# A pairwise bilinear kernel: a third tile for weights loaded twelve pairs ahead, and fields loaded in twos

## The chip, the cores and the metric

One Trainium2 chip, one NeuronCore. The metric is device time in microseconds (us), median of several executions. All runs told here were of the fast state; the runs before of different chips have medians from 760.2 to 761.7 us, so each kernel is also compared with runs of the kernel before on its own chip.

## The reference

There are 1,024 rows of 32 fields with 128 values each, and 496 pairs of fields (i < j), each with its own 128x128 matrix:

```python
v_i = inputs[:, I_IDX, :]
v_j = inputs[:, J_IDX, :]
transformed = jnp.einsum('bpd,ped->bpe', v_i, W)
return transformed * v_j
```

Everything is float32. The output is 260 MB, the weights 32.5 MB, the fields 16.8 MB.

## The kernel before

Pairs are taken with i falling from 30 to 0. All 32 fields stay in SBUF once loaded (4 KB of each partition). For a pair, TensorE multiplies the field by the weights; from pair 15 on with three matmuls of split operands (ScalarE and GpSimd make the split parts). VectorE multiplies by the other field into an output tile of three pairs, and SyncE stores that tile, 1.5 MB in rows of 12 KB. Weights come in tiles of eight pairs, 512 KB in rows of 4 KB, two tiles in turn. Loads go from ScalarE's queue, apart from those of the start:

```python
WL = 8          # pairs in a tile of weights
OG = 3          # pairs in an output tile; four such tiles
WB = 2          # tiles of weights
WLEAD = 6
XLEAD = 5
...
def load_w(c, splits=(0, WL), eng=nc.scalar):
    w_raw[c] = rpool.tile([P, WL, P], F32, tag="w", name=f"w_{c}")
    for a, b in zip(splits, splits[1:]):
        eng.dma_start(out=w_raw[c][:, a:b, :], in_=wt[c, :, a:b, :])
...
w_at = {}
for c in range(WB, -(-NQ // WL)):
    free = (c - WB + 1) * WL if (c - WB) * WL < nq0 else 0
    w_at[max(c * WL - 3 * WC + 1 - WLEAD, free)] = c
...
for u in range(2 * NQ + LAG):          # u: half a pair
    q = u // 2
    if u < 2 * NQ:
        i, j = pairs[q]
        if u % 2 == 0 and j == i + 1 and 0 <= i - 2 - XLEAD:
            load_x(i - 2 - XLEAD, eng=nc.scalar)
        first(u)                        # two matmuls, ScalarE scales PSUM
        if u % 2 == 1 and q in w_at:
            load_w(w_at[q])
    if u >= LAG:
        second(u - LAG)                 # third matmul, VectorE, the store
    ...                                 # one split of weights or of half a field
```

## Time and profile before

| | before |
|---|---|
| median of 6 runs (range) | 761.69 us (760.32 to 763.02) |
| span of the profiled run | 758.7 us |
| HBM read, written | 49.3 MB, 260.0 MB |
| DMA queues busy, of 16 engines | 83.1% + 16.0% |
| ScalarE's wait for weights | 38.7 us, 39 times |
| VectorE's wait for a free output tile | 46.6 us, 49 times |

The page is read for two kinds of facts: how busy an engine is (shares), and who waited for whom. The prediction below shows the lines that carry it. Not shown there are the issues of DMA, on the same page (source and target, the issuing queue, count, KB each, median us from issue to landing):

```profile
out_dram<-ot SPq DMA_DIRECT2D x163, 1536.0 KB, 13.5
w<-in_wt_dram ACTq DMA_DIRECT2D x60, 512.0 KB, 9.0
x<-in_xt_dram ACTq DMA_DIRECT2D x24, 512.0 KB, 9.4
```

A store takes 13.5 us to land although its 1.5 MB move in under 4 us at 409 GB/s: several are queued one behind the other.

### The profile page before, as it was taken

How to read it: one execution, taken by the hardware profiler on the slowest of the kernel's cores; microseconds unless marked ns; L12 is line 12 of the kernel's file. 1: busy time of each engine (PE TensorE's matmuls, PEld its weight loads, DVE VectorE, ACT ScalarE, POOL GpSimd, SP SyncE). 2: the span in 40 equal slices, each digit the busy share in tenths (PEclk: the TensorE clock that was granted, in tenths of full speed). 3: DMA queues.
4: the chain of work that ended last, by engine and by line, in shares of the span. 5: the costliest groups of instructions: out<-in, count | busy, mean ns of one | idle time of the engine just before them, and what ended most of it. 6: DMA issues, size and time to landing. Idle time of an engine off the chain costs nothing.

```text
span 758.7 us, 11264 instructions
## 1 busy us (share of the span) xinstructions
PE 708.1 (93%) x2946; PEld 551.6 (73%) x2946; DVE 633.7 (84%) x1012; ACT 625.7 (82%) x1256; POOL 595.6 (78%) x863
## 2 busy tenths in 40 slices
PE   7979989999999999999998989999999999999992
PEld 3557778777777777777786878778787777777771
DVE  4869989987888779788797989888888888888883
ACT  1368889988888888888887979898899899989881
POOL 0959999999888987978878787888887878786650
PEclk9999999999999999999999999999999999999996
DMA  9999999999999999999999999999999999999996
GB/s 351 427 406 389 425 394 424 427 418 430 420 422 418 425 423 409 419 416 411 400 411 420 404 423 402 422 417 409 410 414 417 402 423 400 408 424 404 416 412 257
DMA packets 38800, 310.07 MB, mean 409 GB/s; under 512 B 4304, under 2 KB 4432, under 8 KB 17872
## 3 DMA queue, kind: packets, MB, share of 16 engines
q1 hardware_dynamic: 26064, 264.25, 83.1%
q10 hardware_dynamic: 12672, 45.09, 16.0%
q8 instruction: 24, 0.39, 0.2%
q14 instruction: 40, 0.33, 0.1%
HBM read 49.28 MB, written 260.05 MB: 408 GB/s over the span
## 4 chain that ended last, share of the span: by engine, by line
DMA 40%; PE 39%; DVE 12%; POOL 5%; issue 1%; ACT 1%; DVEq 0%; ACTq 0%; POOLq 0%
DMA out_dram<-ot 34%; PE po L162 24%; DVE ot L177 12%; PE po L171 12%; DMA w<-in_wt_dram 6%; PE po L159 4%; POOL xl L111 1%; POOL xd L116 1%; POOL wl L96 1%; POOL xl L112 1%; POOL wd L98 1%; ACT po L163 0%; DMA x<-in_xt_dram 0%; DVE xd L203 0%; POOL wd L97 0%
## 5 line engine op out<-in xcount | busy, mean ns | idle before, releaser
L177 DVE TENSOR_TENSOR ot<-po,x 128x512 f32<-128x512 f32 x992 | 619.8, 683 | 109.4 <-DMA out_dram<-ot 46.6
L163 ACT ACTIVATE po<-po 128x512 f32<-128x512 f32 x962 | 540.7, 582 | 58.6 <-PE po L162 24.4
L162 PE MATMUL po<-xh,wh 128*128 128x512 f32 x962 | 382.6, 398 | 13.6 <-DVE ot L177 12.9
L171 PE MATMUL po<-xd,wd 128*128 128x512 f32 x962 | 377.8, 393 | 12.6 <-ACT po L163 11.4
L162 PE MATMUL po<-xl,wl 128*128 128x512 f32 x962 | 378.7, 394 | 5.6 <-POOL wl L96 5.3
L96 POOL TENSOR_TENSOR wl<-w,wh 128x256 fp32r<-128x256 f32 x241 | 181.0, 751 | 76.0 <-ACT wh L95 62.2
L162 PEld LDWEIGHTS po<-xh,wh 128*128 128x128 f32 x962 | 181.8, 189 | 72.0 <-DVE ot L177 33.9
L171 PEld LDWEIGHTS po<-xd,wd 128*128 128x128 f32 x962 | 181.7, 189 | 54.0 <-POOL wd L97 5.7
L162 PEld LDWEIGHTS po<-xl,wl 128*128 128x128 f32 x962 | 182.0, 189 | 46.3 <-POOL wl L96 9.7
L98 POOL TENSOR_TENSOR wd<-wl,wd 128x256 fp32r<-128x256 f32 x241 | 178.4, 740 | 20.1
L95 ACT ACTIVATE wh<-w 128x256 fp32r<-128x256 f32 x241 | 99.8, 415 | 42.3 <-DMA w<-in_wt_dram 38.7
L97 POOL TENSOR_SCALAR wd<-wh 128x256 fp32r<-128x256 f32 x241 | 99.3, 412 | 20.3
L111 POOL TENSOR_TENSOR xl<-x,xh 128x512 fp32r<-128x512 f32 x52 | 69.2, 1331 | 18.6 <-ACT xh L110 18.3
L116 POOL TENSOR_TENSOR xd<-xh,xl 128x512 fp32r<-128x512 f32 x32 | 41.3, 1291 | 2.7
L110 ACT ACTIVATE xh<-x 128x512 fp32r<-128x512 f32 x52 | 32.6, 631 | 12.6 <-DMA x<-in_xt_dram 12.6
L112 POOL TENSOR_SCALAR xl<-xl 128x512 fp32r<-128x512 f32 x52 | 33.3, 641 | 4.6
L159 PE MATMUL po<-x,w 128*128 128x512 f32 x60 | 28.3, 634 | 4.5 <-DMA x<-in_xt_dram 4.5
L159 PEld LDWEIGHTS po<-x,w 128*128 128x128 f32 x60 | 11.8, 202 | 20.2 <-issue 13.0
L203 DVE TENSOR_TENSOR xd<-xh,xl 128x512 fp32r<-128x512 f32 x20 | 16.8, 838 | 3.6 <-POOL xl L112 3.6
L110 ACT ACT_TABLE_LOAD x1 | 1.3, 1283 | 4.6 <-DMA w<-in_wt_dram 4.6
L219 POOL MEMSET const-float32-0.0<- 128x1 f32 x1 | 0.1, 98 | 0.2 <-issue 0.2
L219 POOL MEMSET const-bfloat16-1.0<- 128x1 bf16 x1 | 0.1, 101 | 0.0
(2 smaller groups left out, 0.2 us busy)
## 6 DMA issues: line engine op xcount, KB each, us to landing
out_dram<-ot SPq DMA_DIRECT2D x163, 1536.0 KB, 13.5
w<-in_wt_dram ACTq DMA_DIRECT2D x60, 512.0 KB, 9.0
x<-in_xt_dram ACTq DMA_DIRECT2D x24, 512.0 KB, 9.4
x<-in_xt_dram SPq DMA_DIRECT2D x6, 512.0 KB, 8.5
out_dram<-ot SPq DMA_DIRECT2D x5, 512.0 KB, 11.0
x<-in_xt_dram ACTq DMA_DIRECT2D x4, 256.0 KB, 5.9
out_dram<-ot SPq DMA_DIRECT2D x4, 256.0 KB, 10.1
w<-in_wt_dram SPq DMA_DIRECT2D x1, 512.0 KB, 7.9
```

What stands on the lines that cost most here:

```text
L95: nc.scalar.mul(h, raw, 1.0 - 2.0**-13)
L96: nc.gpsimd.tensor_tensor(l, raw, h.bitcast(F32), ALU.subtract)
L97: nc.gpsimd.tensor_scalar(d, h.bitcast(F32), EPS, 1.0, ALU.mult, ALU.mult)
L98: nc.gpsimd.tensor_tensor(d, l.bitcast(F32), d.bitcast(F32), ALU.subtract)
L111: nc.gpsimd.tensor_tensor(l, x_sb[f][:, s], h.bitcast(F32), ALU.subtract)
L112: nc.gpsimd.tensor_scalar(l, l.bitcast(F32), 1.0 / EPS, 1.0, ALU.mult, ALU.mult)
L116: nc.gpsimd.tensor_tensor(d, h.bitcast(F32), l.bitcast(F32), ALU.subtract)
L159: nc.tensor.matmul(po[u], w_raw[q // WL][:, q % WL, :], x_sb[i][:, s], start=True, stop=True)
L162: nc.tensor.matmul(po[u], w_s[c][t][:, r], x_s[i][t][:, s], start=t == 0, stop=t == 1)
L163: nc.scalar.mul(po[u], po[u], 1.0 + EPS)
L171: nc.tensor.matmul(po[u], w_s[q // WC][2][:, r], x_s[i][2][:, s], start=False, stop=True, skip_group_check=True)
L177: nc.vector.tensor_tensor(ots[g][:, k, s], po.pop(u), x_sb[j][:, s], ALU.mult)
```

## The change

Its intent is that ScalarE never waits for weights: a third tile lets each load start about twelve pairs ahead. The room for it comes from field 0, which is needed last and as left operand only, and is now put into one of the three weight tiles late in the run. The other fields are loaded two at a time, so that a partition's row in HBM is 8 KB in place of 4 KB. Cut to its core (text after @@ says where a cut stands, "..." that lines are left out):

```diff
-WB = 2
-WLEAD = 6
+WB = 3
+WLEAD = 12
+XAFTER = 54
@@ load_x
-        t = xpool.tile([P, n, BT], F32, tag=f"x{f}", name=f"x_{f}")
+        if f == 0:
+            t = rpool.tile([P, WL, P], F32, tag="w", name="x_0").rearrange("p q e -> p (q e)").unsqueeze(1)
+        else:
+            t = xpool.tile([P, n, BT], F32, tag=f"x{f}", name=f"x_{f}")
@@ start, after the loads of the first eight fields
+    load_w(2, eng=nc.sync)
@@ w_at
-        w_at[max(c * WL - 3 * WC + 1 - WLEAD, free)] = c
+        early = 0 if XAFTER < c <= XAFTER + WB else WLEAD - 6
+        w_at[max(c * WL - 3 * WC - 5 - early, free)] = c
+    x_at = XAFTER * WL - 11
...
@@ main loop
-            if u % 2 == 0 and j == i + 1 and 0 <= i - 2 - XLEAD:
-                load_x(i - 2 - XLEAD, eng=nc.scalar)
+            f = i - 2 - XLEAD
+            if u % 2 == 0 and j == i + 1 and f > 0 and f % 2 == 1:
+                load_x(max(f - 1, 1), min(f, 2), eng=nc.scalar)
...
+            if u == 2 * x_at + 1:
+                load_x(0, eng=nc.scalar)
```

More of the change, by code (lines that the diff above doesn't have):

```diff
@@ L144 @@
         free = (c - WB + 1) * WL if (c - WB) * WL < nq0 else 0
-        w_at[max(c * WL - 3 * WC + 1 - WLEAD, free)] = c
+        early = 0 if XAFTER < c <= XAFTER + WB else WLEAD - 6
+        w_at[max(c * WL - 3 * WC - 5 - early, free)] = c
+    x_at = XAFTER * WL - 11
+    assert x_at not in w_at and len(w_at) == NQ // WL - WB
     ctx.enter_context(tc.manual_schedule())
```

## The prediction

> **What bounds the kernel now.** I read the page from the top, then the waits, then a table by stage, then the transfers.
>
> ```profile
> span 758.7 us, 11264 instructions
> ...
> PE 708.1 (93%) x2946; PEld 551.6 (73%) x2946; DVE 633.7 (84%) x1012; ACT 625.7 (82%) x1256; POOL 595.6 (78%) x863
> ...
> DMA  9999999999999999999999999999999999999996
> ...
> DMA packets 38800, 310.07 MB, mean 409 GB/s; under 512 B 4304, under 2 KB 4432, under 8 KB 17872
> ...
> q1 hardware_dynamic: 26064, 264.25, 83.1%
> q10 hardware_dynamic: 12672, 45.09, 16.0%
> ...
> DMA 40%; PE 39%; DVE 12%; POOL 5%; issue 1%; ACT 1%; DVEq 0%; ACTq 0%; POOLq 0%
> ```
>
> PE at 93% looks like the bound, but the two DMA queues together are busy 99.1% of the time of all 16 engines: q1 (SyncE's queue, nearly all of it output) 83.1%, q10 (ScalarE's, weights and fields) 16.0%. The longest part of the chain that ended last is also DMA. The waits show who waits for whom:
>
> ```profile
> POOL wl L96 <- ACT wh L95: 62.2, 85, 6.3
> DVE ot L177 <- DMA out_dram<-ot: 46.6, 49, 1.4
> ACT wh L95 <- DMA w<-in_wt_dram: 38.7, 39, 9.1
> DVE ot L177 <- PE po L171: 35.1, 44, 5.1
> ```
>
> Columns: total us, times, longest. Two of these are of interest. ScalarE waits 38.7 us for weights: this is what the change aims at. VectorE waits 46.6 us for an output tile to be free, so the compute is held back by the stores. Which of the two counts is settled by the table by stage (after the busy times: granted clock, DMA share, GB/s):
>
> ```profile
> 20.00:50.00 30.00, 25.25 (x78) 15.51 (x77) 21.15 (x34) 11.95 (x26) 21.18 (x28) 0.94 1.02 423
> 53.00:55.00 2.00, 2.00 (x11) 1.65 (x10) 2.00 (x4) 2.00 (x5) 1.85 (x3) 1.00 0.64 270
> 55.00:130.00 75.00, 71.32 (x301) 56.63 (x300) 72.41 (x112) 65.04 (x134) 68.76 (x94) 0.98 1.01 408
> 260.00:390.00 130.00, 124.20 (x527) 97.30 (x526) 107.75 (x176) 114.01 (x228) 107.81 (x159) 1.00 1.01 414
> 520.00:650.00 130.00, 127.16 (x549) 101.98 (x548) 110.84 (x182) 117.44 (x235) 104.91 (x157) 1.00 1.01 412
> 730.00:745.00 15.00, 14.15 (x60) 10.81 (x58) 14.47 (x24) 11.93 (x23) 5.65 (x9) 1.00 0.97 407
> ```
>
> The DMA share is 1.00 or more (neighbouring packets overlap by a few ns) in every stage but 53 to 55 us and the last 30 us. Counting stores between issue and landing in the trace, 2.0 are in flight on average from 20 to 130 us and 3.1 from 130 to 730 us. So the DMA engines always have something to write when a weight is late. The kernel is bound by the time its 310 MB take on 16 engines.
>
> **What the Trainium skill says.** "DMA: Bandwidth & Descriptors", section "Specifications", gives a fabric ceiling of 435 GB/s; the mean here is 409, so at most 6% is left. The same page, "Queues, rings and completion order", says that an engine takes turns between the queues with work, packet by packet; the trace agrees: while one load runs beside the stores, its packets start 612 ns apart, close to one 12 KB store packet (460 ns) and one 4 KB load packet (159 ns). A lead therefore reorders traffic and does not add capacity. "Where 436 GB/s comes from" and "Latency and other measured facts" (HBM access 0.2 us on average, 2 us under high load) on that page bear on the stretched load packets below: the longest here is 1.6 us.
>
> **The change part by part.** The order of work on TensorE, VectorE and GpSimd is the same before and after; on ScalarE only the places of loads and of the two field splits beside them move, and SyncE gets one more load. HBM bytes are unchanged.
>
> *8 KB rows.* The trace's packet records give medians of 460 ns for 12,288 B, 159 ns for 4,096 B, 9 ns for the 4 B packet that closes a transfer on each engine, and 309 ns for the few 8,192 B packets that are there (instruction fetches). So a packet costs some 8.5 ns plus 27.2 GB/s. Eleven pairs of fields are loaded together, 128 rows each: 1,408 packets save 2x159-309 = 9 ns, 12.7 us of engine time, over 16 engines 0.8 us. Eleven transfers fewer save 11x16x9 ns/16 = 0.1 us. Sum: -0.9 us.
>
> *Third weight tile, lead of twelve pairs.* Before, the load of a tile is issued about six pairs before its first split; six pairs of 1.5 us are 9 us, and the median landing is 9.0 us. So it lands just in time, and ScalarE waits a little 39 times. Six more pairs add 9 us of slack, and nearly all of the 38.7 us goes, and most of GpSimd's 62.2 us behind ScalarE that comes from it. But an idle ScalarE costs end time only where the stores run dry. Adding up in the trace the time in which fewer than 16 engines have a packet: 2.3 us in the first 4 us, 0.1 us from 4 to 20, 1.1 us from 20 to 130, 2.8 us from 130 to 730, 0.5 us from 730 to 748, the rest after the last data. The only gap of note is at 53.7 us (0.6 us, the 0.64 in the table). It follows a 5.8 us wait of ScalarE for weights that ended at 45.2 us and reached VectorE as a 5.1 us wait. That tile was asked for at 34.8 us (pair 16) and is now asked for at pair 8. So -0.6 us from that gap, and at most 1 us more from small ones, of which I count none.
>
> *Stretched packets.* Packets that took over 6 ns more than the straight line add up to 20.1 us (mean of the 16 engines): 0.6 before 20 us, 3.3 to 130, 4.9 to 390, 11.0 to 730. They come just after reads are issued: in the 0.8 to 4.5 us after a load of weights issued with no other read in flight, 0.31 us on average (41 loads); beside another read, 0.10 us (19 loads). Fields: 0.23 us alone (6), 0.12 us beside others (14). Eleven field loads fewer save about 11x0.15 = 1.7 us; some six weight loads lose the field load that covered them, 6x0.2 = +1.2 us. Net -0.5 us. The part after 390 us, where weights are loaded alone in both kernels, should stay.
>
> *Start and end.* One more weight tile goes on SyncE's queue ahead of the first stores, and a pair's second field comes a field early: about 1 MB, 2.4 us of DMA time, moved forward, none of it added. At the end the reads stop some six pairs earlier. There compute needs about 1.36 us a pair (0.68 us a half on TensorE), stores 1.25 us, so the backlog shrinks by 0.11 us a pair over 25 pairs instead of 19: 2.8 us of a backlog of about 11 us, so no new gap, but perhaps a little at the edges. I take 0.
>
> Sum: -0.9 -0.6 -0.5 = -2.0 us, 762.0 to 760.0 us.
>
> **The rivals.** (1) The weights' wait sets the pace. If ScalarE's 38.7 us were on the path, the time would fall to some 723 to 740. For it: TensorE is 93% busy, and VectorE waits for TensorE 35.1 us. Against it: the DMA share of 1.01, and the floor. Taking the 20.1 us of stretched packets and the 4.5 us of gaps from 4 to 748 us wholly away leaves about 737; no earlier weight can do all that. (2) Contention takes the gain back. An 8 KB row has 40% of the bytes beside a 12 KB store row, a 4 KB row 25%, so a field load pushes stores and, at the start, SyncE's own loads aside; with fewer reads left to fill in later, the stores, only two deep to 130 us, run dry more often. That would cost 1 to 2 us: 761 to 763. (3) Read stalls depend on how deep the reads are queued. If loads that no one waits for fall on better moments, half of the 8.2 us before 390 us could go, for 756 to 757; if the number of stalls is kept and each is longer for 8 KB rows, the time is 761. (4) The ring's slot that field 0 takes late puts three weight tiles back to the old lead: some small waits of ScalarE come back near 650 us, hidden as the others were.
>
> **Range and chances.** The runs before lie between 761.2 and 763.0, so a median is good to about 1 us. The terms are each below 1 us, with perhaps 3 us either way for stalls. Range 756.5 to 763.0, prediction 760.0. Faster by over 2% means below 746.8 and needs rival 1; slower by over 2% means above 777 and a new gap of 15 us, for which nothing speaks.
>
> **What would show it right or wrong.** Right: the wait of ScalarE for weights falls below 10 us, VectorE's wait for output tiles grows in exchange, the DMA share stays 0.99 or more, the gap at 53.7 us is gone, packets fall by about 1,600 and those of field pairs take 309 ns. Wrong in the first step if VectorE's wait for output tiles does not grow and the mean GB/s rises above 415; wrong on stalls if the stretched packets change by more than 4 us; wrong on the start if the first 130 us show new gaps.

## The result, and the profile after

The changed kernel took 757.50 us (6 runs, 757.36 to 757.79) against 761.69 us. The ratio is 0.9946, 95% interval 0.9933 to 0.9959. It is the mean time of one kernel's fast runs over that of the other's of the same rounds, so not quite the ratio of the two medians. That is 4.1 us less where 2.0 were predicted. Part of the 4.1 us is the draw: this median of the kernel before is the highest of the five on record, and beside 25 runs on another chip (below) the difference was 3.3 us. A second thing shows in the runs: those of the kernel before spread over 2.7 us, those of the changed one over 0.4 us.

The page of the changed kernel, the lines that answer to those of before:

```profile
span 755.8 us, 11316 instructions
...
PE 706.6 (93%) x2946; PEld 548.1 (73%) x2946; DVE 625.1 (83%) x1012; ACT 629.6 (83%) x1256; POOL 595.4 (79%) x863
...
DMA packets 37216, 310.07 MB, mean 410 GB/s; under 512 B 4128, under 2 KB 4256, under 8 KB 14880
...
q1 hardware_dynamic: 26208, 264.78, 83.6%
q10 hardware_dynamic: 10944, 44.57, 15.4%
...
DMA 52%; PE 23%; DVE 17%; POOL 3%; issue 1%; ACT 0%; DVEq 0%; POOLq 0%; ACTq 0%
```

The DMA queues are as full as they were (99.0% together), with 1,584 packets fewer. The chain that ended last moves further towards DMA (40% to 52%). Its waits (us in total, times, longest; line 100 is the split of weights on ScalarE, 186 VectorE's multiply):

```profile
POOL wl L101 <- ACT wh L100: 70.4, 96, 1.9
DVE ot L186 <- DMA out_dram<-ot: 61.9, 62, 2.6
ACT po L172 <- PE po L171: 51.5, 63, 10.8
...
ACT wh L100 <- DMA w<-in_wt_dram: 0.5, 1, 0.5
```

ScalarE's 38.7 us for weights are gone, and the same engine now waits 51.5 us for TensorE (24.4 before); VectorE waits 15 us more for output tiles. Idle time has moved, little of it has vanished: with the DMA queues full, work done earlier only waits later. By stage (us, busy of PE, PEld, DVE, ACT, POOL, granted clock, DMA share, GB/s):

```profile
20.00:50.00 30.00, 30.00 (x106) 19.64 (x105) 27.30 (x43) 16.88 (x37) 25.59 (x34) 1.00 1.02 427
53.00:55.00 2.00, 0.97 (x5) 0.45 (x3) 1.50 (x3) 1.59 (x4) 1.82 (x3) 1.00 0.98 414
55.00:130.00 75.00, 70.90 (x300) 55.48 (x301) 68.89 (x110) 65.45 (x133) 69.24 (x94) 1.00 1.01 425
520.00:650.00 130.00, 127.12 (x546) 100.88 (x545) 111.28 (x182) 117.39 (x234) 103.22 (x155) 1.00 1.00 413
```

The stage from 55 to 130 us stands out: the same DMA share of 1.01, but 425 GB/s in place of 408. The share counts an engine as busy while a packet is open, also while the packet waits. So a share of 1.01 does not say that no time is lost. For that the packets themselves have to be counted. I added up, in the packet records of each trace, the time by which packets of the two queues exceed the straight line of the prediction (8.5 ns plus their bytes at 27.2 GB/s) by over 6 ns ("stretched"), and the time in which an engine has no packet ("gap"), both as a mean over 16 engines:

| us | before | changed |
|---|---|---|
| all packets at their median length | 733.4 | 732.5 |
| stretched, 20 to 130 us | 3.3 | 0.7 |
| gaps, 20 to 130 us | 1.1 | 0.2 |
| stretched, 130 to 390 / 390 to 730 us | 4.9 / 10.9 | 6.2 / 9.1 |
| gaps, 130 to 390 / 390 to 730 us | 0.9 / 1.9 | 1.1 / 3.1 |
| stores in flight, mean, 20 to 130 us | 2.0 | 2.9 |
| share of 20 to 130 us with one store or none in flight | 21% | 0% |

The first 130 us give 3.6 us, the rows 0.9 us, the rest takes some back; together 3 us, as the spans say (758.7 to 755.8). In this pair of traces the gain is at the start, and there mostly in stretched packets. The start of the kernel before is not the odd one: it loses 0.03 us in stretched packets for each us, as the kernel does again from 390 to 730 us, with three stores in flight. It is the start of the changed kernel that is unusually clean, at 0.006 us.

### The profile page after: what moved, and what is told of

Same layout as the page of the kernel before. It is cut to its first block, busy times and chain, and to the rows that moved or that the text cites. A ratio compares the mean times of both kernels' runs of the same rounds, so it can differ in the third digit from the quotient of the medians.

```text
span 755.8 us, 11316 instructions
## 1 busy us (share of the span) xinstructions
PE 706.6 (93%) x2946; PEld 548.1 (73%) x2946; DVE 625.1 (83%) x1012; ACT 629.6 (83%) x1256; POOL 595.4 (79%) x863
## 4 chain that ended last, share of the span: by engine, by line
DMA 52%; PE 23%; DVE 17%; POOL 3%; issue 1%; ACT 0%; DVEq 0%; POOLq 0%; ACTq 0%
DMA out_dram<-ot 51%; DVE ot L186 16%; PE po L171 14%; PE po L180 7%; PE po L168 3%; DMA x<-in_xt_dram 2%; POOL xd L121 1%; DVE xd L215 1%; POOL wl L101 1%; POOL xl L116 1%; POOL wd L103 0%; POOL xl L117 0%; POOL wd L102 0%; DVEq L186 0%; ACT po L172 0%
## 5 line engine op out<-in xcount | busy, mean ns | idle before, releaser
L186 DVE TENSOR_TENSOR ot<-po,x 128x512 f32<-128x512 f32 x992 | 612.7, 682 | 116.0 <-DMA out_dram<-ot 61.9
L172 ACT ACTIVATE po<-po 128x512 f32<-128x512 f32 x962 | 547.6, 584 | 92.1 <-PE po L171 51.5
L101 POOL TENSOR_TENSOR wl<-w,wh 128x256 fp32r<-128x256 f32 x241 | 180.7, 750 | 73.6 <-ACT wh L100 70.4
L215 DVE TENSOR_TENSOR xd<-xh,xl 128x512 fp32r<-128x512 f32 x20 | 15.2, 762 | 2.8 <-POOL xl L117 2.8
## 6 DMA issues: line engine op xcount, KB each, us to landing
x<-in_xt_dram ACTq DMA_DIRECT2D x11, 1024.0 KB, 11.9
```

What stands on the lines that cost most here:

```text
L101: nc.gpsimd.tensor_tensor(l, raw, h.bitcast(F32), ALU.subtract)
L172: nc.scalar.mul(po[u], po[u], 1.0 + EPS)
L186: nc.vector.tensor_tensor(ots[g][:, k, s], po.pop(u), x_sb[j][:, s], ALU.mult)
```

## The experiments

All times are medians; in brackets runs and range. My theory after the trace: the start gives most of it, because weights that come in time let the compute get three stores ahead by some 50 us, and the rows give the rest. Rivals: the rows and the fewer loads do it; the lead counts all along; the stretched packets come from the number of reads that start.

**Rows alone**, in the kernel before:

```diff
-            if u % 2 == 0 and j == i + 1 and 0 <= i - 2 - XLEAD:
-                load_x(i - 2 - XLEAD, eng=nc.scalar)
+            f = i - 2 - XLEAD
+            if u % 2 == 0 and j == i + 1 and f >= 0 and f % 2 == 1:
+                load_x(f - 1, 2, eng=nc.scalar)
```

> The kernel before with one edit: later fields loaded in twos with 8 KB rows (field 0 too, beside field 1), two weight tiles and the old lead. Row theory of the prediction: 1,536 packets of 309 ns take the place of 3,072 of 159 ns, about 0.9 us less, 761 us; ScalarE's wait for weights stays near 39 us and the gap at 53 us stays. Rival (fewer starts of a read give the gain): stretched packets fall by 2 us or more and the time falls by 2 to 3 us, to about 759.

Measured: 760.90 us (14, 760.17 to 762.17) beside 760.92 us (59) of before, ratio 1.0005 (0.9995 to 1.0015). The packets at their median length fell by 1.0 us as worked out, but stretched packets of the first stage were 4.2 us (3.3 before) and its gaps 0.8 us. Rows alone gain nothing that can be seen; the rival of fewer starts of a read falls, since twelve field loads fewer did not lower the stretched packets (20.4 us, before 20.0).

**The ring without rows**: the changed kernel with fields loaded singly.

```diff
-            if u % 2 == 0 and j == i + 1 and f > 0 and f % 2 == 1:
-                load_x(max(f - 1, 1), min(f, 2), eng=nc.scalar)
+            if u % 2 == 0 and j == i + 1 and f > 0:
+                load_x(f, eng=nc.scalar)
```

> The changed kernel with fields loaded singly in 4 KB rows: third weight tile, field 0 in the ring, lead of twelve pairs stay. If the early weights give the gain (stretched packets and gaps between 20 and 130 us): 758.5 us, 3 us below before, and rows the last 0.9. If the rows and the fewer field loads give it: 761 us, no more than 1 us below before.

Measured: 758.23 us (22, 757.97 to 762.91; 15 of them below 758.3), ratio 0.9974 (0.9965 to 0.9983). The early weights give 2 to 3 us by themselves. The first stage is as good as in the changed kernel (stretched 0.6, gaps 0.2 us).

**The new lead at the start alone**; from tile 7 on the old lead of six pairs (and the load of field 0 one pair later, so that it does not fall on a load of weights):

```diff
-        early = 0 if XAFTER < c <= XAFTER + WB else WLEAD - 6
+        early = WLEAD - 6 if c <= 6 else 0
-    x_at = XAFTER * WL - 11
+    x_at = XAFTER * WL - 10
```

> The changed kernel with the new lead only for tiles 2 to 6; from tile 7 on the old lead of six pairs. If only the start counts (the trace shows the gain between 20 and 130 us): as the changed kernel, 757.5 us within 0.7, although ScalarE waits 15 to 25 us for weights again. If the lead counts all along: 759 us or more.

Measured: 760.01 us (22, 757.81 to 765.84), ratio 0.9999 (0.9983 to 1.0015). The best five runs lie at 757.8 to 758.0, close to the changed kernel; the others lie anywhere up to 8 us above. So early weights at the start alone gain nothing that the ratio can show: the old lead later still lets the kernel reach a good time, but seldom. The profiled run (763.04 us) was one of the slow ones (ScalarE waits 40.6 us for weights in it, where I expected 15 to 25), and its trace shows what a late load can do. First the waits from 396 to 420 us:

```profile
ACT wh L100 <- DMA w<-in_wt_dram: 5.0, 1, 5.0
PEld po L180 <- POOL wd L103: 4.5, 1, 4.5
...
PE po L180 <- ACT po L172: 4.1, 1, 4.1
```

Then three stretches of the same passage (busy times, granted clock, DMA share, GB/s):

```profile
404.00:410.00 6.00, 1.88 (x9) 1.29 (x8) 2.48 (x4) 1.27 (x3) 5.28 (x7) 1.00 1.00 425
410.90:414.30 3.40, 3.40 (x10) 2.66 (x9) 2.13 (x4) 2.09 (x6) 2.22 (x4) 0.50 0.96 396
416.00:418.50 2.50, 2.50 (x12) 2.06 (x11) 2.50 (x4) 2.28 (x6) 1.53 (x4) 1.00 0.47 182
```

ScalarE waits 5.0 us for weights, TensorE stands for 4.1 us, then its clock is granted at half for 3.4 us, and only after that do the stores run dry: a DMA share of 0.47 from 416 to 418.5 us, seven microseconds after the wait for weights ended at 408.7 us. Whether the stop alone would have done it, without the halved clock, was not separated. The Trainium skill, "TensorE: Matmul & The Clock Gate", section "What's actually happening", says that the clock falls to half after at least one idle window, and that a window is 3413 ns long; the trace agrees with the half, and its stretch at half clock is 3413 ns long. Not every late load ends so, which fits the scatter. How many of the slow runs took this course is not shown: only one was profiled.

**The old start, the new lead later**: tile 2 asked for at pair 8 and tile 3 at pair 16 as before, and tile 2 no longer loaded ahead of the first stores.

```diff
-    load_w(2, eng=nc.sync)
-    for c in range(WB, -(-NQ // WL)):
-        free = (c - WB + 1) * WL if (c - WB) * WL < nq0 else 0
+    for c in range(2, -(-NQ // WL)):
+        free = (c - 1) * WL if c < 4 else (c - WB + 1) * WL if (c - WB) * WL < nq0 else 0
-        w_at[max(c * WL - 3 * WC - 5 - early, free)] = c
+        w_at[max(c * WL - 3 * WC - 5 - early, free) + (c == 4)] = c
```

> The changed kernel with the weights of the start as before (tile 2 at pair 8, tile 3 at pair 16), the new lead from tile 4 on. If only the start counts: 760 to 761 us, with ScalarE's 5 to 9 us waits for weights before 50 us and stretched packets of 2 us or more between 20 and 130 us back. If the lead counts all along: 758 us.

Measured: 759.84 us (14, 757.95 to 762.66), ratio 0.9989 (0.9977 to 1.0001). The waits from 20 to 130 us, of before and of this one, each with the line of ScalarE's wait for weights:

```profile
ACT wh L95 <- DMA w<-in_wt_dram: 18.6, 4, 9.1
```

```profile
ACT wh L100 <- DMA w<-in_wt_dram: 15.4, 2, 9.4
```

The long waits are back, and with them stretched packets of 2.6 us and gaps of 1.5 us in that stage, with one store or none in flight for 15% of it. (The profiled run, 762.01 us, is one of the slower ones.) The start is worth about 2.3 us in the median. But the two best runs, 757.95 and 758.27 us, come close to the changed kernel too, so the old start does not bar a good time either. Neither half of the early loads alone gains clearly (ratios 0.9999 and 0.9989, both intervals hold 1); both together, without the rows, gave 0.9974.

**The changed kernel once more**, on the chip of the next three.

> The changed kernel itself, on one chip with the next three. If the start, the lead and the rows are its whole gain: median 757.5 us, runs within 0.5 us of each other, ratio to before 0.995 to 0.996. If its six runs were a lucky chip: scatter of 2 us or more, as the kernels with one part left out showed, and a ratio near 0.998.

Measured: 757.52 us (5, 757.37 to 757.79) against 760.82 us, ratio 0.9960 (0.9947 to 0.9973). The narrow spread is the kernel's own, not the chip's.

**Weights on SyncE's queue**:

```diff
-                load_w(w_at[q])
+                load_w(w_at[q], eng=nc.sync)
```

> The changed kernel with its weights loaded from SyncE's queue, behind the stores, in place of ScalarE's. Theory that packets are stretched because a load starts on a queue that stood empty (44 weight loads alone, 0.26 us each): on SyncE's queue there is none that starts so, stretched packets fall from 17 us to under 9, time 749 to 752. Rival, that a read of HBM among writes costs this wherever it is queued: stretched packets stay at 15 to 18 us, time 757 to 758. Either way a load lands after the stores ahead of it, 14 to 17 us, which a lead of twelve pairs (18 us) just covers.

Measured: 778.37 us (5, 775.59 to 779.88), ratio 1.0226 (1.0203 to 1.0250). Both theories missed. Its page:

```profile
q1 hardware_dynamic: 34704, 295.71, 94.4%
q10 hardware_dynamic: 2448, 13.63, 4.4%
...
L100 ACT ACTIVATE wh<-w 128x256 fp32r<-128x256 f32 x241 | 99.1, 412 | 8.5 <-DMA w<-in_wt_dram 8.5
...
w<-in_wt_dram SPq DMA_DIRECT2D x61, 512.0 KB, 14.3
```

The loads land in 14.3 us (median), within the lead, and few are late: ScalarE waits for weights three times, 8.5 us in all, and gaps grow by some 5 us. The rest is in the packets: stretched packets double to 35.1 us, and the stores' own 12 KB packets grow from a mean of 467 to 482 ns. A load beside the stores, on a queue of its own, is cheaper than one between them in the same queue. My theory that a read is costly because it starts on an empty queue is wrong; this run turns it round. Why a read among the stores of one queue stretches packets was not measured further.

**Twice as many reads**: each load after the start in two halves, partitions 0 to 63 and then, four pairs later, 64 to 127.

```diff
+    def load_half(c, k):
+        if k == 0:
+            w_raw[c] = rpool.tile([P, WL, P], F32, tag="w", name=f"w_{c}")
+        s = slice(k * P // 2, (k + 1) * P // 2)
+        nc.scalar.dma_start(out=w_raw[c][s], in_=wt[c, s])
...
-                load_w(w_at[q])
+                load_half(w_at[q], 0)
+            if u % 2 == 1 and q - 4 in w_at:
+                load_half(w_at[q - 4], 1)
```

> The changed kernel with each weight load after the start cut into two, partitions 0 to 63 and 64 to 127, the second four pairs later: the same bytes and rows, twice as many starts of a read. Theory of starts: each start costs what one does now, 59 more of 0.26 us or somewhat less, plus 0.5 us of closing packets: 8 to 16 us more, 766 to 773. Rival, that the cost goes with the bytes: 758 us.

Measured: 764.55 us (4, 764.30 to 764.81), ratio 1.0052 (1.0037 to 1.0067), between the two. Stretched packets are 23.5 us, 5 to 7 us above the two traces of the changed kernel: 59 more starts at some 0.1 us each, less than half of what the theory of starts gave. The other part of the loss is 7.4 us of gaps from 390 to 730 us, nearly all after 670 us, where field 0 holds the third tile and the second half comes only two pairs before it is needed: there the weights were late (ScalarE waits for them three times, 11.9 us in all), which this edit should not have mixed in.

**Three output tiles in place of four**, so that mostly two stores are in flight (all three only while VectorE waits for a tile):

```diff
-    opool = ctx.enter_context(tc.tile_pool(name="o", bufs=4))
+    opool = ctx.enter_context(tc.tile_pool(name="o", bufs=3))
```

> The changed kernel with three output tiles in place of four, so that at most two stores are in flight. Theory that shallow stores are what stretched packets and left gaps between 20 and 130 us of before (3.3 and 1.1 us in 110 us at a depth of 2.0, against 0.7 and 0.2 now at 3): both grow all along, by 10 to 25 us, 768 to 783. Rival, that two in flight are enough and the start lost its time to late weights alone: 757 to 760.

Measured: 759.88 us (20, 758.43 to 760.88), ratio 0.9986 (0.9977 to 0.9995): 2.4 us more, not ten. The stage from 20 to 130 us tells why (before, the changed kernel, this one):

```profile
20.00:130.00 110.00, 101.57 (x399) 76.24 (x398) 98.28 (x152) 81.84 (x169) 94.44 (x127) 0.97 1.00 410
```

```profile
20.00:130.00 110.00, 104.88 (x421) 77.81 (x420) 100.18 (x158) 86.56 (x178) 99.38 (x134) 1.00 1.01 426
```

```profile
20.00:130.00 110.00, 99.25 (x384) 72.90 (x383) 93.06 (x145) 79.58 (x163) 91.00 (x123) 0.97 1.00 410
```

With weights in time but stores shallow, the start's loss is back in full: 410 GB/s, stretched 3.2 us, gaps 1.8 us, one store or none in flight for 17% of the stage. After 130 us the mean depth stays at 2.1, but there are hardly any moments with only one store (5% to 390 us, none later), and there the loss is only 1.5 to 2 us above the two traces of the changed kernel. So a mean depth of two does not cost what I had put on it.

The end hides part of this loss. Half of the 16 engines still have packets at 754.8 us here, in the changed kernel at 748.7 us, 6 us earlier; but there one or two engines go on for 5.8 us more, here for 2.2 us. So the 2.4 us of the time stand for about 6 us lost by most engines.

Is it the time with one store or none in flight that costs? From kernel to kernel the loss of the first stage goes with it, by 0.15 to 0.25 us for each (before: 23 us of it, 3.6 us more loss than in the changed kernel; here 19 us, 4.1 us; rows alone 17 us, 4.1 us). Packet by packet it does not show. Sorted by the stores in flight when a packet starts, 0.8 of the 3.3 us stretched in the kernel before fall in the moments with one store, and 2.5 us in those with two; here it is 1.2 and 1.8 of 3.2 us. Of the gaps at most 0.2 us fall in moments with one. And the changed kernel spends 17 us of the stage with two in flight and loses 0.1 us in them. Nor are these the loads' packets alone: stores' packets have 1.5 of the 3.3 us before, and 2.2 of 3.2 us here. So what is shown is that shallow stores at the start bring the loss back with all weights in time; what lengthens a packet there stays open.

The runs so far, of two chips on which the kernel before has medians of 760.92 and 760.82 us (stretched + gaps are added before rounding):

| kernel | median | stretched + gaps, 20 to 130 us | one store or none, 20 to 130 us |
|---|---|---|---|
| before | 760.9 | 4.5 | 21% |
| rows alone | 760.9 | 5.0 | 15% |
| old start, new lead later | 759.8 | 4.0 | 15% |
| changed, three output tiles | 759.9 | 5.0 | 17% |
| new lead at the start alone | 760.0 (best 757.8) | 1.5 | 0% |
| ring without rows | 758.2 | 0.8 | 1% |
| changed, again | 757.5 | 0.9 | 0% |

**Looking for more.** Three kernels tried to gain further. The first stores four pairs at a time:

```diff
-OG = 3
+OG = 4
-    opool = ctx.enter_context(tc.tile_pool(name="o", bufs=4))
+    opool = ctx.enter_context(tc.tile_pool(name="o", bufs=3))
```

> Looking for more: the changed kernel with stores of four pairs (2 MB, 16 KB rows) and three output tiles, the same memory. Packets: 63,488 rows of 4 KB stored as 15,872 packets in place of 21,163 of 12 KB, 5,291x8.5 ns/16 = 2.8 us less. Only two stores in flight, which cost 2.4 us with 1.5 MB stores. Sum: 755.5 to 758. If it is over 759, the coarser hand-over of output tiles to VectorE costs more than the packets save.

Measured: 752.51 us (4), but wrong: I had overlooked that the condition for the last, single stores counts on groups of three, and 1.5 MB stayed unwritten. The next two load weights in 1 MB tiles of 16 pairs, two such tiles, field 0 in a tile of its own; the first with three output tiles, the second with four and half the buffers for split weights.

```diff
-WL = 8
-WB = 3
+WL = 16
+WB = 2
-        w_at[max(c * WL - 3 * WC - 5 - early, free)] = c
+        w_at[max((c - 1) * WL - 3 * WC, free)] = c
-    wpool = ctx.enter_context(tc.tile_pool(name="ws", bufs=4))     # the second alone, with o at 4
+    wpool = ctx.enter_context(tc.tile_pool(name="ws", bufs=2))
...            # also: the first tile's halves loaded apart, x_0 from the pool of fields
```

> Looking for more: weights in tiles of sixteen pairs, two tiles, 8 KB rows, loaded 17 pairs ahead; field 0 in a tile of its own, fields in twos; three output tiles of 12 KB to make room. If stretched packets go with the starts of reads: 28 starts fewer of 0.2 to 0.3 us each, 6 to 8 us less; packets 3,700x9 ns/16 = 2 us less; the two stores in flight 2.4 us more: 751 to 754. If they go with the bytes read: only the 2 us for rows and 2.4 us back: 757 to 760.

Measured: 779.98 us (4, 776.03 to 783.44), ratio 1.0238 (1.0193 to 1.0284). Half as many loads did not halve the stretched packets: they rose to 31.5 us, 0.60 us for a 1 MB load alone (0.28 us for one of 512 KB). The cost goes with the bytes and with what flows beside them more than with the starts. There are also 13.8 us of gaps from 390 to 730 us. The waits of that stretch show a wait that the kernels with smaller tiles do not have:

```profile
ACT po L165 <- POOL wl L96: 14.8, 3, 5.3
```

The first of the three ends at 455.57 us. GpSimd's last read of an old tile of weights ends at 455.09 us, ScalarE issues the next load into it at 455.13 us and only then goes on with its own work. So with two tiles and so long a lead the issue of the load itself waits for the tile, and ScalarE behind it. The three largest groups of gaps, some 11 us together, follow these three waits (from 460, 530 and 700 us).

> As the last, with four output tiles of 12 KB and two in place of four buffers for the split weights to make room. If splitting weights only four pairs ahead is enough: 2.4 us under the last. If TensorE waits for GpSimd instead (its wait for wl above 40 us, stores dry): slower than the last, 760 or more.

Measured: 1068.29 us (4), ratio 1.4002 (1.3940 to 1.4064): GpSimd waits 416.6 us for TensorE to give the buffers of the split weights back. That was no fair trade for an output tile.

The first of them mended:

```diff
-        elif g == 0 or q >= NQ - 1 - OG:
+        elif g == 0 or q >= NQ - OG:
```

> The last but three, mended: its condition for single stores left three pairs of the last group but one unwritten (1.5 MB, 3.7 us of stores), which made it wrong and too fast. With them written: 752.5 + 3.7 = 756.2 us, some 1.3 us under the changed kernel, the 2.8 us that 16 KB rows save less what the coarser stores cost. If it is at 757.5 or over, the gain seen was the missing stores alone.

Measured: 755.76 us (6, 755.27 to 756.32), correct, ratio 0.9935 (0.9914 to 0.9955), the fastest of all:

```profile
span 754.5 us, 11201 instructions
...
DMA packets 31455, 310.06 MB, mean 411 GB/s; under 512 B 3488, under 2 KB 3616, under 8 KB 14368
...
out_dram<-ot SPq DMA_DIRECT2D x122, 2048.0 KB, 12.5
```

Beside the changed kernel (757.5 us, on other chips) that is 1.7 us. 5,761 packets fewer at 8.5 ns are 3.1 us over 16 engines; the stage from 20 to 130 us loses more with three output tiles (stretched 1.9 us, gaps 0.4 us, against 0.9 us for both). The two were not separated.

## Why the prediction was right or wrong

- **The bound.** Right. DMA share stayed at 99%, VectorE's wait for output tiles grew by 15 us as the weights' wait fell, and taking 38 us of waits from ScalarE gave 3.3 to 4.1. Rival 1 needed 22 us or more; it is out. (The 6% left to the fabric ceiling was an estimate from the page's 435 GB/s.)
- **Rows, -0.9 us.** Right in packets (medians sum to 0.9 us less), and in the changed kernel worth 0.7 us by the medians with and without them (or 1.1 us by the two ratios to before; the runs are of different chips). Alone in the kernel before they were worth nothing that could be seen, probably because there another loss sets how far the runs lie above the least time; that was not tested. Terms of this sum do not add freely.
- **The gap at 53.7 us, -0.6 us.** Right in mechanism: the wait for tile 3 is gone and so is the gap. All gaps to 130 us fell by 1.0 us.
- **Stretched packets, net -0.5 us.** This is the step that failed. I laid each stretched packet to the start of a read, gave each start its mean cost and counted starts. Measured is -2.6 us in the first 130 us, and the count of starts does not give it: half the field loads in the kernel before do not lower the cost, twice the weight loads add only 0.1 us for each start, and three output tiles bring 3.2 us back with all weights in time. In its place the runs show that the cost of that stage comes with shallow stores: 2.6 to 4.2 us where 2.0 to 2.1 are in flight on average, 0.6 to 0.8 us in the changed kernel and the ring without rows, where it is 2.7 to 2.9 (and 1.3 us at 2.8 with the new lead at the start alone). I had the depth of 2.0 against 3.1 in my hands and used it only to argue that the DMA never starves. Which moments cost, and why later stages lose as much with three in flight, is open. The later stages moved by +1.2 and -1.9 us, together -0.7 us, which is within what two traces of the changed kernel differ by (1.4 us in all stretched packets).
- **Scatter.** I treated the old kernel's spread as noise. It was the larger part: the least time of the kernel before is 758.68 us in 59 runs on one chip, only 1.3 us over the least of the changed one (of 11 runs; more runs find a lower least), but its median lies 2.2 us above its own least and that of the changed kernel 0.1 to 0.2 us. The kernels with half of the early loads show it: least times of 757.81 and 757.95 us, near the changed kernel's 757.36 us, and medians 2.5 and 2.3 us higher. A lead long enough pays by making the good run the usual run.
- **"Most of GpSimd's 62.2 us behind ScalarE goes."** Wrong: 70.4 us. ScalarE now waits for TensorE (51.5 us) in its program order, no longer for weights, and GpSimd waits behind it. Nothing shows that this cost time.
- **Start and end, 0.** Near enough: no new gap at the start; gaps from 730 to 748 us rose from 0.5 to 0.9 us, so the backlog seems to have thinned out.
- **Rivals 2 to 4.** No contention at the start (rival 2). Stretched packets before 390 us fell from 8.2 to 6.9 us, in the first 130 us alone (rival 3: 1.3 us, not the 4 us that it named; and reads were not queued deeper, 1.4 in flight on average in that stage against 1.5 before). ScalarE waited once for weights in all, 0.5 us (rival 4).
- **Readings.** The longest load packet in the trace before took 2.2 us, and two more took 2.1 and 2.0 us, so "1.6 us" was misread. "Between 761.2 and 763.0" leaves out the sixth run, 760.32 us; the median is 761.69 us, not 762.0.

What stays open: what lengthens packets in the first 130 us and not there in the changed kernel, and how often the course of late load, standing TensorE, halved clock and dry stores was taken in the slow runs.

## What to carry to other kernels

When DMA share is near 100%, look also at the GB/s by stage and at the length of single packets: a stage with the same share and 4% fewer GB/s has something to give, and here it was the first 130 us, where the stores were not yet queued deep enough. The longer lead was needed both there and later: neither part alone gained clearly, and both together made the good run the usual one. So compare the spread and the least time of the runs, not the median alone. Larger rows gained nothing alone here, and 0.7 us once the loads came early.

## What the Trainium skill lacked or had wrong

- "DMA: Bandwidth & Descriptors", section "Issuing engines are not separate DMA queues", says that issuing from several engines only saves sequencer time. Here moving 59 weight loads from ScalarE's queue to the one of the stores cost 2.8% (757.52 to 778.37 us on one chip, stretched packets 17 to 18 us against 35 us, stores' packets 467 against 482 ns). Some 5 us of it are gaps, with a few late loads among their causes; the rest is in longer packets.
- No page says how packets lengthen when stores run shallow: 2.6 to 4.2 us lost in 110 us with 2.0 to 2.1 stores of 1.5 MB in flight on average, against 0.6 to 0.8 us with 2.7 to 2.9.
- No page has a figure for how far apart the 16 engines can end. In the traces of the kernel before and of the changed one, half of them have packets until 751.5 and 748.7 us, and one or two go on for 5.8 us more (to 757.3 and 754.5 us); with three output tiles it is 2.2 us. Which engine it is (packet records carry no engine's number), and whether the fetching of instructions (queues q8 and q14, 0.7 MB) makes it late, is open.
- "TensorE: Matmul & The Clock Gate", section "What's actually happening", ties the halved clock to an idle window of about 3.4 us. Here gaps of 1.8 to 2.9 us in TensorE's work were followed by a window of 3.41 us at 0.50 in several traces (before: a gap of 1.9 us at 405 us, half clock from 408.2 us), and others of 1.8 to 2.5 us were not (before: 2.5 us at 441 us).
